# Causal attentions: each dense projection product as four products on 32 columns of TensorE each

## The chip, the cores and the metric

The kernel runs on one core of a Trainium2 chip. Its engines run side by side, each with its own instruction stream: TensorE (matrix products, called PE in the profile, and PEld for the loading of its stationary operand, the weights), VectorE (DVE), ScalarE (ACT), GpSimd (POOL) and SyncE (SP, which issues transfers). TensorE multiplies a stationary operand, at most 128 rows by 128 columns, with a moving operand of up to 512 columns, and writes to PSUM. The metric is the device time of one execution in microseconds, the median of several runs.

## The reference, cut to what matters

Two layers of a decoder act on x, of shape 8 x 256 x 512 in float32. Each layer has three parts, and each part ends in a residual sum and a layer norm:

```
x = layernorm(x + L0_attn(x))     # differential attention, causal, 32 half heads of 16, 8 key heads
x = layernorm(x + L0_xattn(x))    # long convolution by 8 filters
x = layernorm(x + L0_ffn(x))      # 8 experts, two chosen for each token
x = layernorm(x + L1_attn(x))     # self attention, causal, 16 heads of 32
x = layernorm(x + L1_xattn(x))    # cross attention to a context, with its own keys as well
x = layernorm(x + L1_ffn(x))      # attention, causal, with one routed key and value head for each token
```

Three of these six are causal attentions. Each makes queries, keys and values by dense projections (x @ W.T, the contraction over 512 features), then scores, softmax and the product with the values; the first two also have a dense output projection. Everything is float32.

## The kernel before, in words

The six parts follow one another. The three causal attentions share one function, `causal_attention` (line 1203). It cuts the 2048 tokens into four groups of 512 tokens (two batches of 256 each) and each batch into units of four heads: 8 units for each batch in the differential attention, 4 in the others, so 64, 32 and 32 units. The order of the instructions on TensorE, VectorE, ScalarE and GpSimd is written by hand there, one *slot* for each unit:

- `maxima(u)` (line 1249): 12 score products ps_q of unit u, each on 32 rows of the array (line 1257); ScalarE copies them out (1266), GpSimd masks them (1268), VectorE takes the maxima (1277).
- a *fill*: some steps from a queue of projection work.
- `products(u - lag)` (line 1350): values times weights (1363) and row sums (1373) of an earlier unit, each as products on 32 columns of the array, four beside one another, one for each head; VectorE takes the reciprocal of the sums (1381).
- `weights(u - wait)` (line 1309): 8 score products ps_k on 32 rows each (1320), with 8 small bf16 ones that subtract the maxima (1329); ScalarE takes the exponential (1337), GpSimd clears what lies above the diagonal (1338) and adds two blocks (1348) for the row sums.
- another fill, at times `turn` (1299, small bf16 products by columns), another fill.

A fill takes steps from the queue until a budget in microseconds is spent; the steps' costs are constants (MM = 0.86 for a product with 512 moving columns, TR = 0.45 for four transposes), not measured in the run. What is due at a slot is done by then (`need`). So the order of instructions is fixed when the kernel is built.

The projection steps are made by `product_steps` (line 198): one step is one product k of the four (KB = 4) that sum over the 512 features, into one PSUM tile; after the last step a function `done` copies the tile out or adds it to x. Who calls it: `feature_block` (queries and keys, tile ps_f, 256 or 512 moving columns), `keys` (ps_k in the differential attention), `token_block` (values and the routed keys, ps_t, 512 moving columns) and `out_block` (the output projection, ps_o, 512 moving columns). All their products carry line 205 in the profile. The values of the differential attention (`values`, line 349, tile ps_v, 128 moving columns) go through `project` (line 169), and carry line 172, with many products of other parts that the change leaves alone.

Among these stand transposes on the whole array (line 217 for x and the context, 536, 448, 510 and 1874 for other tiles).

Of the kernel before, what the change touches and what calls it, by code (L numbers as in the profile page):

```python
# [24 lines left out]
P = 128  # L25
# [5 lines left out]
KB = D // P  # L31
# [19 lines left out]
def decoder_kernel(ctx: ExitStack, tc: tile.TileContext, a: dict, out: bass.AP):  # L51
    nc = tc.nc
# [76 lines left out]
    def load_w(slot, at, src, cols, behind=None):  # L129

        view = slot[:, at : at + KB * cols].rearrange("p (k c) -> p k c", k=KB)
        ins = nc.sync.dma_start(out=view, in_=src.rearrange("(k p) c -> p k c", p=P))
        if behind:
            wait_for(ins.ins, behind, "not among the tokens' transfers")
        return view
# [33 lines left out]
    def project(ps, lhsT, rhs, n=KB):  # L169

        for k in range(n):
            nc.tensor.matmul(ps, lhsT=lhsT(k), rhs=rhs(k), start=(k == 0), stop=(k == n - 1))  # L172
# [22 lines left out]

    MM, TR = 0.86, 0.45

    def product_steps(tile, lhsT, rhs, done, cost=MM):

        ps = []  # L200

        def step(k):
            if k == 0:
                ps.append(tile())
            nc.tensor.matmul(  # L205
                ps[0], lhsT=lhsT(k), rhs=rhs(k), start=(k == 0), stop=(k == KB - 1)
            )
            if k == KB - 1:
                done(ps[0])

        return [(cost, lambda k=k: step(k)) for k in range(KB)]
# [27 lines left out]
    def turned_group(work, pools, g):  # L239

        xT = []

        def step(ti):
            if ti == 0:
                xT.append(work.tile([P, KB, GT], F32, tag="xT", name="xT", bufs=1))
            turned(pools, xT[0][:, :, ti * P : (ti + 1) * P], x[g * TPG + ti])

        return xT, [(0, [(TR, lambda ti=ti: step(ti))]) for ti in range(TPG)]
# [28 lines left out]
    def diff_attention():  # L277
# [10 lines left out]
        wv = load_w(w, 2560, a["L0_attn_Wv"], P)  # L288
# [53 lines left out]
        def prepare(work, pools, g, at, here):  # L342
            qT = work.tile([P, KB, GT], F32, tag="qT", name="qT")
            kz = work.tile([P, 2, GT], F32, tag="kz", name="kz")
            v = work.tile([P, TPG, P], F32, tag="v", name="v", bufs=3)
            xT, turns = turned_group(work, pools, g)
            batches = [slice(b * S, (b + 1) * S) for b in range(2)]

            def values(ti, ps=[]):
                if ti == 0:  # L350
                    ps.append(pools.tile([P, TPG, P], F32, tag="mm", name="ps_v"))
                project(
                    ps[-1][:, ti, :],
                    lambda k: xT[0][:, k, ti * P : (ti + 1) * P],
                    lambda k: wv[:, k, :],
                )
                if ti == TPG - 1:
                    nc.scalar.copy(v, ps.pop())

            values_steps = [(MM, lambda ti=ti: values(ti)) for ti in range(TPG)]  # L360

            def keys(tokens):
                def done(ps):
                    for i in range(2):
                        nc.scalar.mul(kz[:, i, tokens], ps, half[:, i : i + 1])

                n = tokens.stop - tokens.start
                return product_steps(
                    lambda: pools.tile([P, n], F32, tag="mm", name="ps_k"),
                    lambda k: wk[:, k, :],  # L370
                    lambda k: xT[0][:, k, tokens],
                    done,
                    MM * n / GT,
                )

            if g:

                need = turns + [(0, values_steps), (0, keys(slice(0, GT)))]
            else:
                need = turns[:2] + [(0, keys(batches[0]))]  # L380
                need += [(3, steps) for _, steps in turns[2:]]
                need += [(8, keys(batches[1])), (9, values_steps)]
            for b, tokens in enumerate(batches):
                for c, first in enumerate((0, 1, 4, 5)):
                    block = feature_block(pools, qT, xT, wq, 0, c, HD0**-0.5, tokens)
                    need.append((8 * b + first, block))
            need.sort(key=lambda piece: piece[0])

            if g == NG - 1:

                for t in range(2):
                    load_context(work, t)
                for t in range(NT):
                    slot = 16 * g + 6 + t
                    at(slot - here, "fill", [(TR, lambda t=t: turn_context(work, pools, t))])
            return (
                need,
                lambda rows, c, at, n: qT[rows, c // 4 * 2 + c % 2, at : at + n],
                lambda rows, c, at, n: kz[rows, c // 2 % 2, at : at + n],
                lambda k, h: v[:, k, 32 * (h % 4) : 32 * (h % 4) + 32],  # L400
            )
# [3 lines left out]
        def load_context(work, t):  # L405
            cx[t] = work.tile([P, D], F32, tag="cx", name="cx")
            nc.sync.dma_start(out=cx[t], in_=cin[:, t, :])

        def turn_context(work, pools, t):
            c = work.tile([P, KB, P], F32, tag="cT", name="cT")  # L410
            turned(pools, c, cx.pop(t))
            nc.sync.dma_start(out=ctx_d[:, :, t * P : (t + 1) * P], in_=c)
            if t + 2 < NT:
                load_context(work, t + 2)
# [1098 lines left out]
    def feature_block(pools, r, xT, w, at, c, scale=1.0, tokens=slice(0, GT)):  # L1513

        cs = slice(at + c * P, at + (c + 1) * P)
        n = tokens.stop - tokens.start
        return product_steps(
            lambda: pools.tile([P, n], F32, tag="mm", name="ps_f"),
            lambda k: w[:, k, cs],
            lambda k: xT[0][:, k, tokens],  # L1520
            lambda ps: nc.scalar.mul(r[:, c, tokens], ps, scale),
            MM * n / GT,
        )

    def token_block(pools, xT, w, at, ti, done):

        return product_steps(
            lambda: pools.tile([P, D], F32, tag="mm", name="ps_t"),
            lambda k: xT[0][:, k, ti * P : (ti + 1) * P],
            lambda k: w[:, k, at : at + D],  # L1530
            done,
        )
# [465 lines left out]
```

## Time and profile before

| | |
|---|---|
| median of 3 runs | 2151.02 us (2148.34 to 2153.92) |
| the profiled execution | 2155.62 us; span from first to last instruction 2153.9 us |
| TensorE, products | 2011.0 us busy (93% of the span), 15094 records |
| TensorE, weight loads | 1222.2 us (57%), 15094 records |
| VectorE | 1272.2 us (59%) |
| GpSimd | 827.1 us (38%) |
| ScalarE | 603.1 us (28%) |
| mean granted TensorE clock | 0.979 |
| line 205, tile ps_f, 256 moving columns, self attention | 512 records, 126.2 us |
| line 205, tile ps_t, 512 moving columns, routed attention | 256 records, 123.0 us |
| lines 1363 and 1373, by columns | 2048 and 1152 records |

A record of the profile is one instruction with its start and length. A float32 product has two records on TensorE and two weight loads, so the 852 products that the change touches (788 of line 205, 64 of tile ps_v) are 1704 records. The form "128*32 128x256 f32" reads: 128 rows by 32 columns of the array in use, a moving operand of 128 partitions and 256 columns, in float32. Products are pipelined: a record's length (0.59 us at 512 columns) is longer than the distance to the next start, so the distance between starts tells what a product costs the stream. "Busy" counts the union of lengths, and so covers part of the time in which the array only drains or waits for weights. In the views by stretch of time the six parts lie at 0 to 465, to 806, to 1104, to 1463, to 1804 and to 2154 us.

### The profile page before, as it was taken

How to read it: one execution, taken by the hardware profiler on the slowest of the kernel's cores; microseconds unless marked ns; L12 is line 12 of the kernel's file. 1: busy time of each engine (PE TensorE's matmuls, PEld its weight loads, DVE VectorE, ACT ScalarE, POOL GpSimd, SP SyncE). 2: the span in 40 equal slices, each digit the busy share in tenths (PEclk: the TensorE clock that was granted, in tenths of full speed). 3: DMA queues.
4: the chain of work that ended last, by engine and by line, in shares of the span. 5: the costliest groups of instructions: out<-in, count | busy, mean ns of one | idle time of the engine just before them, and what ended most of it. 6: DMA issues, size and time to landing. Idle time of an engine off the chain costs nothing. (4 is left out here: it accounts for less than half of the span.)

```text
span 2153.9 us, 36055 instructions
## 1 busy us (share of the span) xinstructions
PE 2011.0 (93%) x15094; PEld 1222.2 (57%) x15094; DVE 1272.2 (59%) x1935; ACT 603.1 (28%) x765; POOL 827.1 (38%) x919
## 2 busy tenths in 40 slices
PE   8989999879998999999969999998999999999995
PEld 6545655444443455656646665656787884444453
DVE  4677777658888963222236756555334333576787
ACT  4545555520010022211124433330110111333342
POOL 3677777736556722000034544333000000243343
PEclk9989999989999999999989999999999999999997
DMA  6899702234133154231132210002100100000000
GB/s 230 332 402 402 300 2 61 84 101 186 35 105 134 30 158 146 67 144 64 44 100 63 84 60 31 2 1 99 40 24 16 40 0 1 1 11 11 11 21 30
DMA packets 110033, 197.58 MB, mean 92 GB/s; under 512 B 7088, under 2 KB 30768, under 8 KB 109872
## 3 DMA queue, kind: packets, MB, share of 16 engines
q1 hardware_dynamic: 104752, 178.49, 23.5%
q0 software_dynamic: 5120, 16.78, 2.3%
q8 instruction: 121, 1.98, 0.4%
q14 instruction: 40, 0.33, 0.0%
HBM read 93.54 MB, written 112.20 MB: 96 GB/s over the span
## 5 line engine op out<-in xcount | busy, mean ns | idle before, releaser
L1381 DVE RECIPROCAL rsum<-ps_pv 128x256 f32<-128x256 f32 x128 | 224.5, 1754 | 238.0 <-PE ps_pv L1373 238.0
L172 PE MATMUL ps_y<-kv,wt 128*128 128x512 f32 x640 | 278.9, 594 | 5.4 <-DVE kv L590 2.7
L1337 ACT ACTIVATE pT<-ps_k 128x1536 f32<-128x1536 f32 x128 | 185.7, 1451 | 271.2 <-PE ps_k L1329 267.4
L1277 DVE TENSOR_REDUCE neg<-rows 128x12 f32<-128x1536 f32 x128 | 223.0, 1742 | 40.1 <-POOL rows L1268 40.1
L1266 ACT COPY rows<-ps_q 128x1536 f32<-128x1536 f32 x128 | 184.1, 1438 | 180.4 <-PE ps_q L1257 122.0
L1338 POOL TENSOR_SCALAR_AFFINE_SELECT pT<-pT 128x1024 f32<-128x1024 f32 x128 | 141.2, 1103 | 242.8 <-ACT pT L1337 242.8
L1268 POOL TENSOR_SCALAR_AFFINE_SELECT rows<-rows 128x1024 f32<-128x1024 f32 x128 | 141.5, 1105 | 221.8 <-ACT rows L1266 221.6
L172 PEld LDWEIGHTS ps_y<-kv,wt 128*128 128x128 f32 x640 | 120.0, 190 | 156.2 <-issue 136.6
L1348 POOL TENSOR_TENSOR pT<-pT 128x512 f32<-128x512 f32 x112 | 145.3, 1298 | 9.3
L1182 POOL DMA_INDIRECT w_l1x<-ys,slots x32 | 33.3, 1040 | 265.0 <-DMA ys<-y_m 257.4
L205 PE MATMUL ps_f<-xT,w_l1a 128*128 128x256 f32 x512 | 126.2, 394 | 0.9 <-ACT xT L218 0.9
L205 PE MATMUL ps_t<-w_l1f,xT 128*128 128x512 f32 x256 | 123.0, 615 | 0.0
L205 PEld LDWEIGHTS ps_f<-xT,w_l1a 128*128 128x128 f32 x512 | 95.0, 193 | 20.4 <-issue 4.6
L1090 PE MATMUL po_m<-dn,hT 128*128 (+1 forms) x216 | 98.8, 594 | 1.5 <-ACT hT L1080 1.5
L140 POOL TENSOR_SCALAR rstd<-bn_mv 128x1 f32<-128x1 f32 x80 | 16.7, 209 | 209.0 <-DVE bn_mv L146 203.2
L1373 PE MATMUL ps_pv<-pT,ones_v 128*32 128x256 f32 (+1 forms) x1152 | 87.5, 387 | 8.7 <-POOL pT L1348 8.4
L628 DVE TENSOR_REDUCE yc<-z 128x64 f32<-128x512 f32 x128 | 86.2, 674 | 5.6 <-issue 5.2
L1257 PE MATMUL ps_q<-kz,qT 32*128 32x128 f32 x1536 | 61.5, 289 | 15.9 <-ACT pT L1337 13.4
L172 PE MATMUL pg<-gu,xT_b 128*128 x216 | 71.5, 467 | 4.6 <-issue 3.7
L1069 DVE TENSOR_TENSOR h_b<-h_b,pg 128x352 f32<-128x352 f32 x36 | 18.7, 521 | 94.8 <-ACT h_b L1068 94.8
L1257 PEld LDWEIGHTS ps_q<-kT,qT 32*128 32x128 f32 x1536 | 49.8, 190 | 42.1 <-issue 19.5
L205 PEld LDWEIGHTS ps_t<-w_l1f,xT 128*128 128x128 f32 x256 | 45.9, 192 | 47.6 <-issue 44.8
(338 smaller groups left out, 3696.0 us busy)
## 6 DMA issues: line engine op xcount, KB each, us to landing
xs<-zero SPq DMA_DIRECT2D x8, 4352.0 KB, 33.2
ys<-zero SPq DMA_DIRECT2D x8, 4352.0 KB
filters<-in_L_xattn_k SPq DMA_DIRECT2D x4, 2560.0 KB
first_h<-xs SPq DMA_DIRECT2D x36, 256.0 KB, 2.7
ys<-y_m SPq DMA_DIRECT2D x36, 256.0 KB, 2.0
gu<-in_L_ffn_gate_up_proj SPq DMA_DIRECT2D x3, 2816.0 KB, 16.2
wt<-filters SPq DMA_DIRECT2D x32, 256.0 KB, 2.6
x<-in_x SPq DMA_DIRECT2D x16, 256.0 KB, 5.5
```

The lines of the kernel that those rows point to most:

```text
L172: nc.tensor.matmul(ps, lhsT=lhsT(k), rhs=rhs(k), start=(k == 0), stop=(k == n - 1))
L205: nc.tensor.matmul(ps[0], lhsT=lhsT(k), rhs=rhs(k), start=(k == 0), stop=(k == KB - 1))
L1090: nc.tensor.matmul(po, lhsT=hT[:m, i, :], rhs=dn[i][:m, bass.ds(e, 1), :], start=(i == 0), stop=(i == len(FCH) - 1),)
L1257: nc.tensor.matmul(block[:, s, j, :], lhsT=q(rows, c, b * S + i * P, P), rhs=k(rows, c, b * S + keys * P, P), start=True, stop=True,)
L1266: nc.scalar.copy(d.rearrange("p j s k -> p s j k"), block)
L1268: nc.gpsimd.affine_select(out=rows, in_=rows, compare_op=ALU.is_ge, fill=-FAR, base=0, pattern=[[0, 8], [-1, P]], channel_multiplier=1,)
L1277: return lambda: nc.vector.tensor_reduce(neg[u // upb % 2][:, :, :, c], d, AX.X, ALU.max, negate=True)
L1337: nc.scalar.activation(p[:, 0:3].rearrange("p j s q -> p s j q"), block, AF.Exp)
L1338: nc.gpsimd.affine_select(out=p[:, 0:2].rearrange("p j s q -> p (j s) q"), in_=p[:, 0:2].rearrange("p j s q -> p (j s) q"), compare_op=ALU ...
L1348: nc.gpsimd.tensor_tensor(p[:, 3], p[:, 1], p[:, 2], ALU.add)
L1373: nc.tensor.matmul(ps[32 * s : 32 * s + 32, 1, j * P :], lhsT=ones_v, rhs=p[:, 1, s, :] if j else first[:, :, s, :], start=(j == 0), stop= ...
L1381: nc.vector.reciprocal(r, ps[:, 1, :])
```

## The change

Each of those products becomes four: the stationary operand's 128 columns are cut into four slices of 32, and each slice writes its 32 partitions of the same PSUM tile. The four read the same moving operand. The fill's costs stay as they are, and so does the order of the steps; no other engine's instructions change.

```
+    def by_columns(ps, lhsT, rhs, start, stop):
+
+        for s in range(4):
+            cs = slice(32 * s, 32 * s + 32)
+            nc.tensor.matmul(ps[cs], lhsT=lhsT[:, cs], rhs=rhs, start=start, stop=stop)
+
     def product_steps(tile, lhsT, rhs, done, cost=MM):
...
-            nc.tensor.matmul(
-                ps[0], lhsT=lhsT(k), rhs=rhs(k), start=(k == 0), stop=(k == KB - 1)
-            )
+            by_columns(ps[0], lhsT(k), rhs(k), k == 0, k == KB - 1)
...
             def values(ti, ps=[]):
...
-                project(
-                    ps[-1][:, ti, :],
-                    lambda k: xT[0][:, k, ti * P : (ti + 1) * P],
-                    lambda k: wv[:, k, :],
-                )
+                for k in range(KB):
+                    by_columns(
+                        ps[-1][:, ti, :],
+                        xT[0][:, k, ti * P : (ti + 1) * P],
+                        wv[:, k, :],
+                        k == 0,
+                        k == KB - 1,
+                    )
```

## The prediction

> **What bounds the kernel now.** I read the stages first (busy time by stretch), then TensorE's own order of time, then what it waits for. The six stretches are the grouped differential attention, the long convolution, the experts, the self attention, the cross attention and the routed attention. The change touches only lines 205 and 172 (tile ps_v) in the first, fourth and sixth.
>
> ```profile
> 0.00:465.00 465.00, 414.01 (x5570) 259.41 (x5570) 315.15 (x362) 239.46 (x245) 299.81 (x301) 0.98 0.59 215
> ...
> 1104.00:1463.00 359.00, 350.36 (x3240) 221.31 (x3241) 218.29 (x282) 136.02 (x169) 160.50 (x178) 0.99 0.14 42
> ...
> 1804.00:2154.00 350.00, 313.56 (x2964) 160.55 (x2964) 239.97 (x336) 116.98 (x116) 117.61 (x124) 0.95 0.04 13
> ```
>
> The columns are length, then busy time of TensorE, its weight loads, VectorE, ScalarE and GpSimd, then granted clock, DMA share and GB/s. TensorE is busy 89%, 98% and 90% of the three stretches; no other engine passes 70%. So what TensorE spends decides here, nearly fully in the self attention and less in the other two. The next view is TensorE's order of time inside one slot (start, length, operation, rows*columns of the array, moving shape, count), and its weight loads in the same stretch:
>
> ```profile
> 299.46 0.59 PE L205 MATMUL ps_o<-w_l,yT_b 128*128 128x512 f32 x1
> 299.99 0.86 PE L1363 MATMUL ps_pv<-pT,v 128*32 128x256 f32 x16
> 300.66 0.61 PE L1373 MATMUL ps_pv<-pT,ones_v 128*32 128x256 f32 x8
> 301.20 0.71 PE L1320 MATMUL ps_k<-qT,kz 32*128 32x256 f32 x8
> 301.74 0.29 PE L1329 MATMUL ps_k<-negT,take 32*128 32x256 bf16 x4
> 301.85 0.40 PE L1320 MATMUL ps_k<-qT,kz 32*128 32x128 f32 x8
> 302.07 0.23 PE L1329 MATMUL ps_k<-negT,take 32*128 32x128 bf16 x4
> 302.24 2.84 PE L205 MATMUL ps_o<-w_l,yT_b 128*128 128x512 f32 x6
> ```
>
> ```profile
> 302.24 0.30 PEld L205 LDWEIGHTS ps_o<-w_l,yT_b 128*128 128x128 f32 x2 [0.16 <-issue]
> 302.77 0.19 PEld L205 LDWEIGHTS ps_o<-w_l,yT_b 128*128 128x128 f32 x1 [0.24 <-issue]
> 303.20 0.19 PEld L205 LDWEIGHTS ps_o<-w_l,yT_b 128*128 128x128 f32 x1 [0.24 <-issue]
> 303.63 0.19 PEld L205 LDWEIGHTS ps_o<-w_l,yT_b 128*128 128x128 f32 x1 [0.24 <-issue]
> ```
>
> Two things are to be seen. First, an f32 product is two records, and one record of 512 columns takes the stream 0.43 us (302.77 to 303.20). Second, the array is used in three forms: whole (128*128), by rows (32*128) and by columns (128*32), and every change of form costs. Line 1363 is already what the change makes of the projections: four products on 32 columns each. Its 16 records and the start of line 1373 lie 0.67 us apart; taken singly they start in fours, 6.7 ns apart, the fours 0.24, 0.216, 0.109 and 0.109 us apart. Whole-array records of 256 columns are also 0.216 us apart, of 128 columns 0.111. Four records side by side thus take what one whole record takes: **the stream does not get longer by itself.**
>
> **The change, part by part.**
>
> (1) The stream. 852 products change (788 of line 205, 64 of ps_v): 1704 whole records become 1704 fours, 5112 records and 5112 weight loads more. By the pitches above, 792 records at 0.429, 784 at 0.216 and 128 at 0.111 make 523 us before, and the same after: 0. Weight loads go from 190 ns for 128 columns to 106 to 110 ns for 32, four within 20 ns (line 1363); both lie behind the running product. If that cover fails, rival A gives the price.
>
> (2) Changes of form. From all pairs of neighbouring TensorE records (starts minus the pitch of the first, medians, nearly without spread): whole to rows or columns 93 ns, rows to whole 110, columns to whole or rows 113. Then the first record of a stretch waits for its own weights: its second comes 105 ns late for whole products (302.24 to 302.77 is 0.53, not 0.43) and for rows, 24 ns for columns, 55 for transposes. No trace shows rows to columns into a projection, but rows into line 1363 and line 1299 cost 110, so I take 110 + 24. With "projection" moving from whole to columns, and counts of the neighbours in the three stretches:
>
> - rows then projection: 110 + 105 becomes 110 + 24: -81 ns, 180 times: -14.6 us
> - projection then rows: 93 becomes 113: +20 ns, 109 times: +2.2
> - line 1363/1373 then projection: 113 + 105 becomes 0: -218 ns, 31 times: -6.8
> - projection then line 1363 (or 1299, 497): 93 + 24 becomes 0: -117 ns, 105 times: -12.3
> - transposes then projection: 0 becomes 93 + 24: +117 ns, 30 times: +3.5
> - projection then transposes: 0 becomes 113 + 55: +168 ns, 27 times: +4.5
>
> The sum is -23.4 us: 9.2 in the first attention, 8.4 in the self attention, 6.1 in the routed one, 0.3 given back at its neighbours. The row that carries this is the gap at 301.20 and 302.24 above. The Trainium skill's "TensorEngine Tiling (Array Packing)", section Key Properties, says that changing the tiling mode, not just the tile, drains TensorE; the 93 to 113 ns here agree. It would make the same sum.
>
> (3) What of it reaches the end. TensorE still waits at places, and a saving made after the start of the chain it waits for is lost there:
>
> ```profile
> PE ps_q L1257 <- ACT pT L1337: 13.4, 13, 1.6
> PE ps_pv L1373 <- POOL pT L1348: 8.1, 20, 0.5
> ```
>
> (first attention, from 50 us to 450; total, times, longest.) The second is the chain ps_k, exponential, GpSimd's select and sum, then line 1373: in a slot that ends in this wait, projections done in between faster only lengthen the wait. I walked through all waits over 130 ns and took off the savings made since the product that starts the chain: 3.9 us of 9.2 in the first attention, 1.2 of 8.4 in the self attention, 2.0 of 6.1 in the routed one. 16.4 us are left. Slots that have under 0.2 us of slack will begin to wait; I take 1.4 for them (estimate), so **-15 us**. Bounds: nothing reaches the end (0), all does (-23.4).
>
> (4) Small things. A product's fourth column block starts 20 ns after its first, so its copy out is 20 ns later: 213 products, at most 4.3 us, hidden where TensorE goes on with other work, taken as 0. No wait is added: the four share the wait that the one had. Instructions: q8 has 121 packets of 16 KB, 0.9 to 2.3 us each, some 9 to 10 us apart in the first attention; TensorE's instructions grow by 34%, so about 6 to 7 us apart at the densest: still hidden, 0. The granted clock: it halves after windows in which TensorE streamed under about 0.37 of the time, and windows with 0.40 of rows and columns alone kept 1.0 (372 us), so products by columns count as work; 0. No DMA, pool or order on another engine changes.
>
> Against the profiled execution, 2155.62 us (span 2153.9): 2140.6. It lies 4.6 us above the median of the runs, 2151.02, so on their scale **2136**.
>
> **Rivals.**
>
> A, slower: the fours do not overlap in a long stream as in line 1363. Its mechanism is a price at each four, once per record that was: the stagger of the four (3 x 6.7 = 20 ns) if a tile's next product waits for the last tile's, 34 us for 1704 fours; or the 24 ns that the first four of each stretch pays, 41 us. It decides from 9.6 ns per four (16.4 us / 1704). Net +18 to +25: 2169 to 2176. For it: the longest stretch by columns in this trace has some six fours, none of 512 columns beyond a second (line 178: 0.453 us, the first interval of a stretch), and none in which four f32 products read one common operand. Against it: of 410 intervals between fours of 256 columns the median is 0.216. The Trainium skill's "TensorEngine Tiling (Array Packing)", section Instruction Overhead, gives about 60 cycles of overhead for each matmul; at its 2.4 GHz 5112 records more would be 128 us (an estimate from that page). The trace's fours, 6.7 ns apart and hidden, speak against that.
>
> B, far slower: the two records of a product come one after the other for each tile, so that only neighbours overlap. Then a product takes four record lengths, not two: +523 us, 2.66 ms. Every four in this trace starts together, with halves in separate fours, so I give it little.
>
> C, no change: the waits of (3) eat it all, since VectorE and GpSimd chains (reciprocal 1.75 us, select 1.1, sum 1.3 per slot) set the slot. Against it: in the self attention TensorE is busy 98%. Time 2151, or 2146 if only the self attention gains 5.
>
> D, the change does all of it: 2127.6.
>
> **How the numbers follow.** Forecast and D together (faster by over 0.3%, 6.5 us, about what a measurement of this kernel can tell from no change) 0.73; C within 0.3% 0.11; A 0.13; B 0.03. The low end is D less half the spread of the runs (2.8 us): 2125. The high end takes C and small forms of A: 2158; above it lie A at full price and B, some 0.14.
>
> **What would show it.** Right: line 205's records become 128*32 in fours 0.429 us apart at 512 columns and 0.216 at 256; no gap between projections and line 1363; rows into projections cost 0.164 then +24 ns; the self attention's stretch shrinks by 6 to 8 us, the others by 4 to 5 each; PE busy falls. Wrong: fours 0.45 apart (A), or line 205's records in ones (B), or equal stretches with longer waits for pT (C). A lower granted clock in the three stretches would be something I did not see coming.

## The result and the profile after

The change takes 2131.53 us (2129.64 to 2133.02, six runs) against 2151.19 us of before: ratio 0.9911, interval 0.9898 to 0.9923. Timed once more, against before again, it was 0.9927 (0.9912 to 0.9942). Forecast were 2136 us, -15 us; measured were -19.1 us (interval -21.9 to -16.6) and -15.7 us (-18.9 to -12.5).

The stretches of time first, with the columns as before; the second and third rows are cut to where the self attention and the routed attention now lie.

```profile
0.00:465.00 465.00, 410.22 (x7226) 235.69 (x7230) 316.07 (x363) 239.74 (x245) 300.80 (x301) 0.97 0.59 216
1095.00:1448.00 353.00, 341.21 (x5552) 176.71 (x5552) 219.46 (x285) 137.24 (x171) 161.51 (x181) 0.99 0.15 45
1783.00:2131.00 348.00, 307.01 (x4128) 137.40 (x4128) 242.68 (x343) 117.89 (x116) 118.54 (x126) 0.96 0.04 14
```

More records (7226 instead of 5570 in the first row), less busy time on TensorE, much less on its weight loads (235.69 for 259.41), and no other engine with notably more to do. Then TensorE's order of time in the slot that the prediction showed, and the weight loads there:

```profile
295.56 1.06 PE L202 MATMUL ps_o<-w_l,yT_b 128*32 128x512 f32 x8 [0.92 <-DVE yT_b L549]
296.45 0.83 PE L1370 MATMUL ps_pv<-pT,v 128*32 128x256 f32 x16
297.10 0.61 PE L1380 MATMUL ps_pv<-pT,ones_v 128*32 128x256 f32 x8
297.64 0.71 PE L1327 MATMUL ps_k<-qT,kz 32*128 32x256 f32 x8
...
298.51 0.23 PE L1336 MATMUL ps_k<-negT,take 32*128 32x128 bf16 x4
298.67 2.78 PE L202 MATMUL ps_o<-w_l,yT_b 128*32 128x512 f32 x24
301.27 1.05 PE L202 MATMUL ps_f<-xT,w_l 128*32 128x256 f32 x16
```

```profile
298.67 0.16 PEld L202 LDWEIGHTS ps_o<-w_l,yT_b 128*32 128x32 f32 x8 [0.16 <-issue]
299.13 0.13 PEld L202 LDWEIGHTS ps_o<-w_l,yT_b 128*32 128x32 f32 x4 [0.30 <-issue]
```

Line 202 is line 205 of before; lines behind the values (line 349 of before) are 7 higher. A *four* is four records side by side, one on each block of 32 columns. The 24 records of ps_o from 298.67 to 301.27 are six fours in 2.60 us: five intervals of 0.429 and a first one of 0.453, against 2.68 us for six whole records. From the first of eight records at 295.56 to line 1370 it is 0.89 us, that is 0.453 + 0.429: no gap at all at this border, where it was 0.09 before. From all neighbouring pairs, the medians are those forecast, to a nanosecond: fours 429, 216 and 109 ns apart, rows to projection 220 - 111 = 109 (f32) and 164 - 54 = 110 (bf16, at half of the 109 that 256 columns take), projection to rows 542 - 429 = 113, projection to line 1370 0, line 1380 to projection 0, transposes to projection 202 - 109 = 93, first interval +24. A *border* is a place where TensorE changes its form; it costs the draining and the wait for the first weights. Counted with these prices, the borders sum to:

| part | borders before | us | borders after | us |
|---|---|---|---|---|
| first attention | 325 | 60.0 | 298 | 50.9 |
| self attention | 172 | 32.4 | 139 | 24.0 |
| routed attention | 173 | 32.1 | 152 | 26.0 |

TensorE waits more than before, as forecast. In the first attention, 50 to 450 us (total, times, longest):

```profile
PE ps_q L1264 <- ACT pT L1344: 13.4, 12, 1.6
PE ps_pv L1380 <- POOL pT L1355: 10.5, 24, 0.6
```

The second was 8.1 us in 20 waits. All idle time of TensorE together is 54.8 us in the first attention (51.0 before), 23.5 in the self attention (22.0), 31.1 in the routed one (28.7).

One difference between the two profiles is not of the change. The span shrank by 23.5 us, and 6.6 of these lie in the experts, from the first gate product to the last down product (309.4 to 302.8 us). In the profile of before TensorE stands still there once, and then runs at half clock for 3.4 us:

```profile
835.73 3.08 PE L172 MATMUL pg<-gu,xT_b 128*128 x6 [3.73 <-issue]
```

The first experiment tells whether that belongs to the kernel before.

### The profile page after: what moved, and what is told of

It reads as the page before. It is cut to its first block, busy times and chain, and to the rows that moved or that the text cites. A ratio compares the mean times of both kernels' runs of the same rounds, so it can differ in the third digit from the quotient of the medians.

```text
span 2130.4 us, 46282 instructions
## 1 busy us (share of the span) xinstructions
PE 1985.9 (93%) x20206; PEld 1127.1 (53%) x20206; DVE 1272.5 (60%) x1935; ACT 604.1 (28%) x765; POOL 828.1 (39%) x919
## 5 line engine op out<-in xcount | busy, mean ns | idle before, releaser
L202 PE MATMUL ps_f<-xT,w_l1a 128*32 128x256 f32 x2048 | 121.7, 384 | 0.7 <-ACT xT L222 0.7
L202 PE MATMUL ps_t<-w_l1f,xT 128*32 128x512 f32 x1024 | 120.7, 603 | 0.0
L202 PEld LDWEIGHTS ps_f<-xT,w_l1a 128*32 128x32 f32 x2048 | 62.1, 110 | 45.2 <-issue 7.0
L1264 PEld LDWEIGHTS ps_q<-kz,qT 32*128 32x128 f32 x1536 | 50.7, 193 | 44.3 <-ACT pT L1344 31.8
L1327 PE MATMUL ps_k<-qT,kT 32*128 32x256 f32 (+1 forms) x1024 | 67.9, 351 | 4.2 <-ACT rows L1273 3.0
## 6 DMA issues: line engine op xcount, KB each, us to landing
xs<-zero SPq DMA_DIRECT2D x8, 4352.0 KB, 32.4
```

The source lines that it names most:

```text
L202: nc.tensor.matmul(ps[cs], lhsT=lhsT[:, cs], rhs=rhs, start=start, stop=stop)
L1264: nc.tensor.matmul(block[:, s, j, :], lhsT=q(rows, c, b * S + i * P, P), rhs=k(rows, c, b * S + keys * P, P), start=True, stop=True,)
L1327: nc.tensor.matmul(block[:, s, at, :], lhsT=k(rows, c, b * S + j * P, P), rhs=q(rows, c, b * S + j * P, P * (2 - j)), start=True, stop=False,)
```

## The experiments

My theory: the stream is as long as before, and the gain is the sum of changes of form that vanish or get cheaper, less what waits take. Its rivals: the gain comes from shorter weight loads or from products by columns as such; or the three attentions are not independent of one another. Ratios are to before, timed on the same chip.

**Before, once more** (no edit).

> The kernel before once more, unchanged, for a second profile of it. Between the two profiles at hand the experts' stretch is 6.5 us shorter after the change, though no instruction of it changed. Theory (that is a transfer that came late in the one profiled execution of before): here the stretch from the first gate product to the last down product is shorter than the 309.3 us of the first profile, near 303, and the span is near 2147 to 2150. Rival (the change reaches the experts in some way): 309 again.

The experts' stretch is 302.9 us here, span 2150.0, and the still-stand is not there. Of all profiles of this study most have 302.8 or 302.9, some 306.6 to 308.3, and the first profile of before 309.4, with whole products and with columns alike. So it comes and goes without the change (what makes it was not found), and a comparison by stretches is needed to keep it out. This is also why the two spans differ by more than the medians.

**One attention at a time.** A name is noted at the start of each attention, and the form chosen by it (for the values of the first attention likewise):

```
-            by_columns(ps[0], lhsT(k), rhs(k), k == 0, k == KB - 1)
+            form = by_columns if part[0] in ("a",) else whole     # ("s",), ("r",) in the other two
+            form(ps[0], lhsT(k), rhs(k), k == 0, k == KB - 1)
```

> Only the first attention's projections by columns, the other two on the whole array. Theory (counted changes of form, less what waits take): -5 us against before (9.2 counted, 3.9 lost in waits), first attention's line 202 records in fours. The profile of the change itself showed only 2 us less at the end of this attention. Rival (this stretch is bound by GpSimd and ScalarE): 0 to -2.

> Only the self attention's projections by columns. Theory: -8.4 counted, 1.2 lost in waits, so -7 to -8.5 us against before, all of it between the first and the last projection of the self attention (353.3 us before, 345 here). Rival (the gain needs all three, or lies outside the attentions): under 4.

> Only the routed attention's projections by columns. Theory: -6.1 counted, 2.0 lost, so -4 to -6 us against before. The three runs with one attention each should add up to the change's -19.7. Rival: a sum well under that, were the parts not independent.

| by columns | ratio, interval | us |
|---|---|---|
| first attention only | 0.9976 (0.9966 to 0.9985) | -5.2 |
| self attention only | 0.9966 (0.9955 to 0.9978) | -7.3 |
| routed attention only | 0.9969 (0.9956 to 0.9981) | -6.7 |
| sum | | -19.1 |

The sum is the change's -19.1. Each of the three is known to 2 or 3 us, and the change's second timing gave -15.7, so within some 4 us the parts are independent. First and self attention are as counted (5.3 and 7.2 left after waits); the routed one gains more than the 4.1 counted.

In the profiles the first attention's gain doesn't show at once. It ends at 466.6 to 470.5 us in four profiles with whole products there, and at 461.6 to 468.3 in four with columns; in the profile of the run with this attention alone by columns it is 467.6. The time that TensorE spends at half clock in it varies as much: 14.7 to 23.9 us with whole products, 15.2 to 35.8 with columns. At half clock records of 256 columns lie 0.427 us apart, not 0.216, so up to half of that time is lost. With half of it taken off (an estimate), the attention ends at 456.5 to 459.3 and at 450.4 to 454.0: 5 us less on the mean.

In the routed attention, from the cross attention's last product to the end, it takes 353.8 us in four profiles with whole products (354.2 in a fifth) and 347.8 to 348.3 in five with columns. TensorE's idle time grew by 2.4 us there, about as taken off. But the time at half clock within the stretch fell from about 34 us (31.9 in the fifth) to 28.6 to 28.9: at the tail, where TensorE mostly waits, one or two of the 3.4 us pieces in which the clock is recorded fewer came out slow. At most half of such time is lost, 2.6 us. That would be what was missing in the count, but it is not shown: the profile with 31.9 us was no shorter than the other four.

**Two halves, not four quarters**: 64 columns each.

```
-        for s in range(4):
-            cs = slice(32 * s, 32 * s + 32)
+        for s in range(2):
+            cs = slice(64 * s, 64 * s + 64)
```

> Each projection product as two on 64 columns, not four on 32. The stream stays as long, the weight loads are shorter than whole ones, but the form is not that of lines 1370 and 1380, so a change of form stays at each border. Theory (the gain is borders that vanish): counted with 50 ns for a first weight load of 64 columns, -55 ns x 180 (rows to projection), +20 x 109, -55 x 31, +20 x 105, +143 x 30, +168 x 27 = about +1 us, so 0 against before within 4 us, and +19 against the change. Rival (the gain is shorter weight loads, or columns as such): half of the change's gain, -10 us.

Ratio 0.9974 (0.9964 to 0.9984), -5.6 us (-7.7 to -3.4): neither my 0 within 4 us nor the rival's -10. The prices could now be read:

```profile
299.57 0.23 PE L1336 MATMUL ps_k<-negT,take 32*128 32x128 bf16 x4
299.73 2.79 PE L202 MATMUL ps_o<-w_l,yT_b 128*64 128x512 f32 x12
302.36 1.90 PE L202 MATMUL ps_f<-xT,w_l 128*64 128x256 f32 x16
304.18 0.30 PE L1306 MATMUL ps_n<-ident_b,terms 128*32 128x128 bf16 x8
```

The six pairs of 512 columns take 2.63 us, that is 0.480 + 5 x 0.429: a first weight load of 64 columns costs 51 ns. The eight pairs of 256 columns take 0.10 us more than 8 x 0.216, for the change from halves to quarters. From all neighbouring pairs, rows to halves cost 110 ns, halves to rows or quarters 100, not 113. (Counted from the last record to start, not from the first of its pair or four, leaving halves, quarters or whole products costs 93 ns alike: a pair is spread over 7 ns, a four over 20.) With these prices the count is -1.4 us, nearly all of it in the self attention.

By stretches the self attention took 352.3 us, as with whole products (352.2 to 353.3 in five profiles); with quarters it is 344.6 to 347.4 in seven. The routed one took 351.2 us (353.8 with whole products), again with the half clock at 28.7 us. The rest lies in the first attention, 466.3 us, within what it varies with whole products. So about 4 of the 5.6 us are no counted border; the half clock may have part in them. The weight loads were shorter here too, and stream and neighbours the same:

```profile
L202 PEld LDWEIGHTS ps_f<-xT,w_l1a x1024: 132/137/232, 1104.0 to 1405.6; 128*64 128x64 f32 x171
```

(shortest, median and longest in ns.) Over the self attention the weight loads were busy for 181.6 us, with whole products 218.9, with quarters 173.5. So halves bring most of what quarters save in weight loads, and at most 1 us of time; quarters, which have the form of line 1370, bring 5 to 9. In the self attention, then, the gain is in the borders. Behind the row of weight loads stands the Trainium skill's "TensorE: Matmul & The Clock Gate", section LDWEIGHTS (loading the stationary operand): the time goes by columns, one for each cycle at 1.2 GHz. The shortest loads here, 186, 132 and 106 ns for 128, 64 and 32 columns, are that slope (54 and 26 ns, the page's 53 and 27) on some 80 ns that it does not have.

**The cross attention too**, where whole products have no neighbours by columns. All its products go through the same four slices:

```
-                project(
+                columns(
                     ps[:, i, :],
                     lambda k: rows[n][:, k, i * P : (i + 1) * P],
...
+    def columns(ps, lhsT, rhs, n=KB):
+
+        for k in range(n):
+            by_columns(ps, lhsT(k), rhs(k), k == 0, k == n - 1)
```

> The change, and the cross attention's products by columns as well. There the neighbours are transposes on the whole array alone. Theory: 11 borders from transposes at +117 ns and 10 to transposes at +168 ns, so the stretch from its first product to its last gets 3 us longer (334.1 us in both profiles at hand), and the whole is 2134 to 2135 us. Rival (columns are faster by themselves): the stretch gets shorter by some us, as its weight loads take 110 instead of 190 ns.

Ratio 0.9961 (0.9947 to 0.9975), -8.4 us: 7 to 11 us of the change's gain are gone, where 3 were expected. The stretch grew from 334.1 to 340.4 us, more than the 3 counted but in the direction that speaks against columns as such. The 21 borders cost 3.0 us by the prices, fours stayed 216 and 429 ns apart, and the waits within grew (lines are 12 higher than in before here):

```profile
PE ps L202 <- DVE ts L1665: 4.1, 1, 4.1
PE ps L202 <- ACT xT L116: 1.9, 1, 1.9
PE ps_o L202 <- ACT yT_x L1736: 1.7, 4, 0.8
```

In the change these are 2.3, 1.9 and 0.7 us. All idle time of TensorE in the stretch grew from 4.1 to 6.8 us, with the same 6.8 us at half clock in both. So borders and waits make 5.7 of the 6.3 us. (In before the first wait is 4.0 us and the stretch still 334.1, but there only 3.4 us ran at half clock.) What the median lost beyond the stretch is 1 to 4 us, by the timing of the change that one takes; this stays unexplained (the profiled execution was the fastest of the five, 2139.3 us, though its experts took 306.6).

**Without GpSimd's addition**, on before and on the change. In the first attention TensorE sums the rows of both blocks of weights, as it already does in the last batch:

```
-                late = u >= units - upb
-                spare = late and u % 2
+                late = u >= units - upb or gather is not None
+                spare = u >= units - upb and u % 2
...
-                if u < units - upb:
+                if u < units - upb and gather is None:
                     nc.gpsimd.tensor_tensor(p[:, 3], p[:, 1], p[:, 2], ALU.add)
```

> The kernel before, but in the first attention the row sums are taken by TensorE from both blocks of the weights (as it does in the last batch anyway), so that GpSimd's addition of the blocks, 1.3 us a unit, goes. It computes the same. TensorE gets 8 records of 128 columns a unit more, 0.22 us, 12 us over 56 units; the waits of line 1373 for GpSimd (8.1 us from 50 to 450 us) should go. About 2150 to 2156 us. It is the base for the next run.

> The same edit on the change. Theory (GpSimd's chain takes the first attention's gain): without the addition the first attention gains 7 to 9 us against the run with the same edit on before, not 2 to 5. Rival (the gain there is lost to something else, such as ScalarE's exponential that the score products wait for): 2 to 5 us again.

One execution each: 2148.35 us on before, under the 2150 to 2156 expected, and 2134.96 on the change. The first attention took 464.0 us on before and 459.9 on the change, 4.1 less: the rival's side. TensorE's idle time there grew from 42.6 to 46.4 us, as much as with the addition (51.0 to 54.8). A second profile of the edit on the change (the last run below) has 458.8 and 44.9 us, which makes it 5.2 less and 2.3 more idle; that too is under the 7 to 9 of my theory. So the addition is where the longest queue of waits stood, but when it goes other waits still take a part of the saving, some 2 to 4 us. My theory of one absorbing chain falls. I had not expected that the edit would make the first attention shorter in both kernels, though TensorE has more to do.

**The loops turned**, so that neighbours are on the same columns. All four steps are issued with the last (the values, tile ps_v, keep their order):

```
-            by_columns(ps[0], lhsT(k), rhs(k), k == 0, k == KB - 1)
+            if k == KB - 1:
+                for s in range(4):
+                    cs = slice(32 * s, 32 * s + 32)
+                    for i in range(KB):
+                        nc.tensor.matmul(
+                            ps[0][cs], lhsT=lhsT(i)[:, cs], rhs=rhs(i), start=(i == 0), stop=(i == KB - 1)
+                        )
```

> The change with its loops turned: all four steps of a projection are issued with the last one, and for each block of 32 columns the four products over k come one after another, so that neighbours in the program are on the same columns. It computes the same. Theory (products run side by side only if neighbours in the program are on different columns): no overlap but between the last of one block and the first of the next, so a projection takes nearly four times as long, the stream of 523 us becomes some 2000 us, and the whole 3600 us. Rival (TensorE or what orders its program finds the products that fit beside one another): about the time of the change, 2130 to 2140.

2887.8 us in one run, 756 us over the change: neither of the two. The trace shows the last block of one product (ps_f) beside the first of the next (ps_t):

```profile
2316.29 0.62 PE L215 MATMUL ps_t<-w_l1f,xT 128*32 128x512 f32 x1
2316.72 0.59 PE L215 MATMUL ps_f<-xT,w_l1f 128*32 128x512 f32 x1
2316.75 0.59 PE L215 MATMUL ps_t<-w_l1f,xT 128*32 128x512 f32 x1
2317.14 0.59 PE L215 MATMUL ps_f<-xT,w_l1f 128*32 128x512 f32 x1
2317.18 0.59 PE L215 MATMUL ps_t<-w_l1f,xT 128*32 128x512 f32 x1
```

Each block has eight records 0.43 us apart, but a new block starts every 1.75 us, so the second four records of one lie beside the first four of the next. Two blocks run at a time, not four. A projection that stands alone takes five times four lengths, where fours need eight: 2.5 times the stream. Projections in a row share the overlap, as the lines show, and come near 2 times. From each projection record's start to the next record's, without idle time, TensorE spent 557 us in the change and 1227 here: 670 of the 756 us. Idle time grew by 35 us; the rest was not taken apart. So the order of the loops is what makes the change harmless: four neighbours on four different columns.

**Whole products next to transposes.** The 128 products for which the prices say so go back to one product; the rest stays by columns:

```
+        n = count[0]
+        count[0] += 1
+        if any(a <= n < b for a, b in WHOLE):
+            nc.tensor.matmul(ps, lhsT=lhsT, rhs=rhs, start=start, stop=stop)
+            return
         for s in range(4):
```

> The change, but the 128 of the 852 products that stand next to transposes, where whole products cost less by the counted borders, are whole again. By the same prices 4.2 us less than the change, of which some is lost in waits: 2128 to 2131, that is 1 to 3.5 us under the change (2131.5), and -21 to -23 against before. Rival (the borders at transposes cost nothing that counts): the same as the change.

2132.27 us, ratio 0.9917 (0.9902 to 0.9931), -17.8: not to be told from the change (0.9911 and 0.9927), and short of the -21 to -23 expected, though its interval just reaches -21. The borders fell by 4.1 us as priced. The first and the self attention are within their spread, and the routed one is 1.4 us longer, with 33 us at half clock. The run cannot say whether the borders at transposes count in the three attentions; in the cross attention they did.

**The change again, and with the additions gone, timed.**

> The change once more, unchanged, timed beside the next kernel on the same chip: -19 to -20 us against before, as first measured, and a third look at the stretches (first attention near 466, self attention 363, routed attention 348 us).

> The change with the first attention's row sums taken by TensorE from both blocks, as in the run with one look, now timed. In single looks the edit made the first attention 4.4 us shorter on before (468.4 to 464.0) and 6.5 us on the change (466.4 to 459.9), though TensorE gets 12 us of work more there: what GpSimd's addition held up is worth more. Theory: 4 to 6.5 us under the change, 2125 to 2128, the fastest of all. Rival (the looks were chance: in four looks with whole products the first attention varied from 466.6 to 470.5): within 2 us of the change.

The change: 2134.09 us against 2148.15, ratio 0.9927, that is -15.7, short of the -19 to -20 expected; its self attention took 344.9 us. With the addition gone: **2125.13 us, ratio 0.9893 (0.9875 to 0.9912)**, 7 to 9 us under the change, more than the 4 to 6.5 expected, and the fastest of all. Its first attention takes 458.8 us (466.4 and 468.3 in the change's two profiles), and TensorE's stretch to 460 us reads, the change first:

```profile
0.00:460.00 460.00, 407.69 (x7212) 234.90 (x7212) 315.37 (x361) 239.33 (x244) 299.40 (x301) 0.97 0.60 218
```

```profile
0.00:460.00 460.00, 413.92 (x7678) 250.78 (x7678) 312.82 (x367) 239.63 (x245) 229.90 (x247) 0.99 0.60 218
```

GpSimd has 70 us less to do. TensorE's idle time in the attention is 44.9 us, not 54.8 and 55.5, and its time at half clock 13.7, not 27.1 and 35.8: half-clock time is work done at half speed, so it can cost up to half its length on top of the idle time. That the waits for the addition bring the half clock about would fit this, but was not tested by itself, and two profiles with the addition have as little: 14.7 us in the run with the self attention alone by columns, 15.2 in the one with the cross attention too.

## Why the prediction was right

- **The stream** (1): as said. Fours are 0.429, 0.216 and 0.109 us apart in the change, in long stretches by columns too. Rival A (a price at each four) and rival B (no overlap) are out; the turned loops show what it takes to come near B.
- **Changes of form** (2): each price was met to a nanosecond or two, the one that no trace had shown included (rows to columns into a projection, 110 + 24). Counted with these prices, borders fell by 23.6 us in the three attentions, for 23.7 forecast.
- **What reaches the end** (3): idle time of TensorE grew by 3.8, 1.5 and 2.4 us in the three attentions, for 3.9, 1.2 and 2.0 taken off. In the first attention four profiles each, with whole products and with columns, have 51.0 to 52.9 and 54.8 to 57.5 us. No run shows that the further 1.4 us for slots with little slack were needed. GpSimd's chain, the one that I described as the taker, was only in part the cause: with its addition gone, other waits still took 2 to 4 us.
- **Small things** (4): the weight loads stayed hidden. Instruction packets grew from 121 to 161, and no wait of TensorE for them shows. The clock was said to be unmoved; it was not quite. In the routed attention 5 us less ran at half clock, worth up to 2.6 us. That attention beat its count by as much (6.7 for 4.1), which fits but is not shown. In the first attention the granted clock reads 0.97 for 0.98, one of the signs that I had not seen coming; the time at half clock there varies by 9 us between profiles of whole products alone, so it can't be put down to the change.
- **The signs**: the self attention's stretch is 7 to 9 us shorter, the routed one's 6, a little over what I named. The first attention's 4 to 5 come out of the timing and, in the profiles, only after the half clock is taken off.
- **Rival C** (nothing reaches the end) is out by the three separate runs, each clear of 1. **D** (all of it) lies at 2127.6, under every run of the change.

So the mechanism was right, and so was the sum of the borders. That -15 came within 1 us of the second timing is partly luck: the 1.4 us that no run shows and the half clock that I left out lie on the same side, and without these two errors the sum would be about -19, as in the first timing. The two timings of the same kernel differ by 3.4 us, so the runs can't decide between them.

## What to carry to other kernels

Count TensorE's changes of form, not only its products: here 670 borders cost 125 us of 2150 by the prices, and a product could be put in its neighbours' form at no cost to the stream, as long as the products that share the array follow one another in the program. Do it where the neighbours have that form; next to transposes on the whole array it costs at both ends (117 and 168 ns here). And where TensorE waits in many short pieces for another engine, giving TensorE that engine's work can pay even when TensorE is the busiest: it paid 7 to 9 us here.

## What the runs showed of the hardware

- Four f32 records of 128 moving columns on different column blocks run in 0.109 us, one every 27 ns, with their starts 7 ns apart, so more instructions alone cost nothing here. (The Trainium skill's 60 cycles a product, in "TensorEngine Tiling (Array Packing)", Instruction Overhead, are not seen as a cost of the 2556 products more.)
- Leaving a form costs 93 ns after the last record for halves, quarters and whole products alike, about 90 for rows, and a first weight load costs 24, 51 or 105 ns beyond the stream for 32, 64 or 128 columns (55 for transposes).
- Of products on the same columns, the second half of the records runs beside the first half of the next block's, 30 ns apart. I had expected only the last product of a block beside the first of the next; whether TensorE or what laid out its program does that is not settled.
